# Attention values on quarters of the array, with the keys in block order 3, 2, 0, 1

## The chip, the cores and the metric

The kernel runs on one core of a Trainium2 chip. A core has TensorE (matrix products into PSUM), VectorE, ScalarE and POOL (GpSimd) for the elementwise work, and SyncE (SP), whose queue here issues most DMAs. Each engine takes its instructions in program order. The metric is the device time of one launch in microseconds; the time of a version is the median of several runs. The array of TensorE has 128 rows (contraction) and 128 columns (outputs); an instruction may use all of it, 128 x 64 (a half by columns), or 64 x 64 (a quarter). A float32 product is two matmul instructions.

## The reference

Eight sequences of 256 tokens with 128 features go through a gated cross attention and a gated mixture of experts, both on normalised inputs and added to the input:

```
q = layernorm(x) @ Wq + bq ; k = ctx @ Wk + bk ; v = ctx @ Wv + bv      # 16 heads of 64
scores = q @ k.T / 8 ; masked keys: -1e30 ; keys after the query's position: -1e30
x = x + tanh(g_xattn) * (softmax(scores) @ v @ Wo + bo)
x = x + tanh(g_ffn) * experts(layernorm(x))        # 8 experts 128-512-128, the router's best one
                                                   # does its rows, all others add their constant
```

The context has 1601 keys, but a query at position s sees keys 0 to s only, so the first 256 keys matter. Where every visible key of a query is masked, the softmax is uniform over all 1601 keys. The kernel keeps two extra columns beside the scores for that (`U0`, `U1`, value `NEG_ALL`): their exponentials give the share of the mean value, which `residual` adds.

## The kernel before, in words

**Tiling.** Sequences go in four pairs (`NPAIR`), heads in eight pairs `c` (`NC`). One step `g = 8 * pair + c`, of 32, does two heads of two sequences. All is float32 apart from the bias products, which are bf16. The 256 queries of a sequence are two tiles of 128: tile 0 has blocks 0 and 1 of 64 tokens, tile 1 has blocks 3 and 2, in this order (`load_x`). Keys lie in order 0, 1, 2, 3.

**A step** is software-pipelined over three steps of the loop `for g in range(NG)` (L1254). In iteration `g`:
- `turn(g-2, i)` (L597) transposes the probabilities of head and sequence `i` in three 128 x 128 products and VectorE copies them (L605). Four of them are spread over the step.
- `query(g+1)`, `key(g+1)` (L481, L488): one product of 512 columns each, evicted by ScalarE. `value(g+2)` (L499): the same for the values of four head pairs. These three and others take PSUM banks from the pool `misc` of two.
- `beside_scores` (L1183), after the fourth turn: the product of attention and `wo` of the pair before (`attention_out`, L655), its eviction with the residual (`evict_out`), statistics, transpositions for the next pair, the router.
- `biases(g)` (L516): eight products on quarters of the array put causal and padding biases of query tile 0, and the extra column, into both score banks. `scores(g, b)` (L530) for sequence `b`: eight products on quarters; rows of the array by head `j`, columns by half tile `u`. `tensor_reduce` finds the maximum of tile 0, and two `tensor_tensor_reduce` add the bias to tile 1 and find its maximum (L549, L551).
- `exps(g, 0)` follows scores of sequence 0 at once; `exps(g, 1)` is done in the next iteration, in two parts around the key's eviction (L572). Each exponential instruction is followed by a read of its sum.
- `normalized(g-1, b)` (L583): VectorE's reciprocal and two multiplications on POOL, for both sequences after the third turn.
- `values(g-2)` (L627): the values of both sequences as sixteen instructions of 128 x 64 shape (L616), a head on each half of the array's columns; VectorE adds the bias (L634; ScalarE in the last steps).

Each score bank pair `banks[b]` holds, for each head, columns: an unused one, `U0`, tile 0's scores from `K0` (128), tile 1's from `K1` (256), and `U1`. `U1` and the never visible parts are set once by VectorE's memsets in `plain_constants` (L239 to L242) and stay.

**Order.** All is in an order written out by hand (`tc.manual_schedule()`, L1228). The prologue loads through SP's queue (`load_x`, `load_c`, weights, masks, L124 to L175) and ScalarE's; the sums over the context beyond 256 keys are accumulated by POOL's DMAs (`add_keys`, L154), one after the other in iterations 0 to 6, starting from the load in L164. The epilogue `last_turns` (L1044) ends the last two steps and routes the last pair, beside the planning of the experts' chunks (`plan_full`), and `experts` runs the experts on sorted tokens.

## Time and profile before

| | |
|---|---|
| median of 9 runs | 365.69 us (363.3 to 368.06) |
| the profiled execution | 367.58 us, span 365.9 us |
| TensorE's mean granted clock | 0.985 |
| TensorE busy | 338.3 us |
| VectorE, ScalarE, POOL busy | 248.3, 207.8, 215.8 us |
| span of the loop's steps 0 to 31, first bias product to the last scores | 16.5 to 284 us |
| values (L616, tile o) | 480 instructions, 45.6 us |
| scores (L541) | 1024 instructions, 41.9 us |
| exponentials (L572) | 256, 105.4 us, and as many reads of sums |

How to read it: the page gives the busy time of each engine over the span, and a row of 40 slices with the busy share in tenths. In a timeline a row is start, duration, engine, line, operation, output<-inputs and the number of instructions merged; brackets give the idle time of that engine before it and what ended it. `sc` are the score banks, `o` the values' PSUM tile, `pt` the transposed probabilities, `nmax` the negated maxima, `arena` holds `attT`, the contexts and the weights.

### The profile page before, as it was taken

How to read it: one execution, taken by the hardware profiler on the slowest of the kernel's cores; microseconds unless marked ns; L12 is line 12 of the kernel's file. 1: busy time of each engine (PE TensorE's matmuls, PEld its weight loads, DVE VectorE, ACT ScalarE, POOL GpSimd, SP SyncE). 2: the span in 40 equal slices, each digit the busy share in tenths (PEclk: the TensorE clock that was granted, in tenths of full speed). 3: DMA queues.
4: the chain of work that ended last, by engine and by line, in shares of the span. 5: the costliest groups of instructions: out<-in, count | busy, mean ns of one | idle time of the engine just before them, and what ended most of it. 6: DMA issues, size and time to landing. Idle time of an engine off the chain costs nothing.

```text
span 365.9 us, 9265 instructions
## 1 busy us (share of the span) xinstructions
PE 338.3 (92%) x3244; PEld 238.1 (65%) x3244; DVE 248.3 (68%) x857; ACT 207.8 (57%) x743; POOL 215.8 (59%) x315
## 2 busy tenths in 40 slices
PE   8978799999999999999999999999998698889993
PEld 3434466667667766667766556677577476888893
DVE  3588889785767778887766887756877755724331
ACT  2276587765555757575564875743955414445452
POOL 6065467582365778768764645865848814335654
PEclk9999999999999999999999999999999989989997
DMA  6789666797799994000000000000760039489800
GB/s 182 212 171 205 106 106 102 114 293 229 213 388 383 386 384 175 2 4 1 2 17 0 17 31 1 2 17 2 301 265 17 31 97 322 122 242 364 326 24 15
DMA packets 36472, 53.69 MB, mean 147 GB/s; under 512 B 3946, under 2 KB 22974, under 8 KB 36425
## 3 DMA queue, kind: packets, MB, share of 16 engines
q1 hardware_dynamic: 28280, 44.00, 35.7%
q0 software_dynamic: 7360, 8.73, 12.5%
q8 instruction: 26, 0.43, 0.5%
q10 hardware_dynamic: 784, 0.36, 0.4%
q14 instruction: 22, 0.17, 0.2%
HBM read 27.82 MB, written 25.71 MB: 146 GB/s over the span
## 4 chain that ended last, share of the span: by engine, by line
PE 60%; DVE 16%; DMA 9%; ACT 6%; issue 3%; SPq 2%; POOL 1%; ACTq 0%; POOLq 0%; DVEq 0%
PE pt L603 8%; PE k L491 7%; PE o L616 6%; PE hs L986 6%; PE y L660 6%; DVE sc L551 5%; PE sc L541 5%; PE v L506 5%; PE ys L1002 5%; ACT prob L572 4%; PE q L484 4%; DMA g_sb<-in_g_xattn_dram 2%; DVE nmax L549 2%; DMA arena<-in_ctx_dram 2%; DVE arena L634 2%
## 5 line engine op out<-in xcount | busy, mean ns | idle before, releaser
L572 ACT ACTIVATE prob<-sc,nmax 128x129 f32<-128x129 f32 (+1 forms) x256 | 105.4, 426 | 92.3 <-DVE nmax L551 65.6
L595 POOL TENSOR_TENSOR prob<-prob,rs 128x256 f32<-128x256 f32 (+1 forms) x128 | 104.2, 901 | 58.9 <-DVE rs L586 57.5
L603 PEld LDWEIGHTS pt<-ident,prob 128*128 128x128 f32 x384 | 46.7, 141 | 55.9 <-issue 45.3
L605 DVE COPY probT<-pt 128x384 f32<-128x384 f32 x128 | 67.2, 546 | 11.5 <-PE pt L603 11.1
L603 PE MATMUL pt<-ident,prob 128*128 128x128 f32 x384 | 64.6, 279 | 4.4 <-DVE probT L605 2.9
L551 DVE CUSTOM_DVE_ANT_0 sc<-sc,bias 128x256 f32<-128x256 f32 x128 | 55.3, 432 | 4.5 <-DVE nmax L549 0.2
L572 ACT ACTIVATION_READ_ACCUMULATOR prob<-sc,nmax 128x1 f32 x256 | 53.8, 210 | 0.0
L616 PE MATMUL o<-probT,v 128*64 128x256 f32 x480 | 45.6, 332 | 0.0
L541 PE MATMUL sc<-kT,qT 64*64 64x256 f32 (+3 forms) x1024 | 41.9, 298 | 0.0
L616 PEld LDWEIGHTS o<-probT,v 128*64 128x64 f32 x480 | 29.7, 136 | 16.8 <-issue 7.0
L491 PE MATMUL k<-cT,arena 128*128 128x512 f32 x64 | 35.5, 636 | 4.8 <-DVE arena L634 3.8
L506 PE MATMUL v<-arena,cT 128*128 128x512 f32 x64 | 33.1, 601 | 1.7 <-ACT qT L486 1.6
L484 PE MATMUL q<-xT,arena 128*128 128x512 f32 x64 | 33.1, 598 | 0.1
L541 PEld LDWEIGHTS sc<-kT,qT 64*64 64x64 f32 x1024 | 31.6, 134 | 0.1
L1020 POOL DMA_INDIRECT out_dram<-o,rows x18 | 17.6, 980 | 22.1 <-DVE o L1013 15.9
L549 DVE TENSOR_REDUCE nmax<-sc 128x2 f32<-128x258 f32 x64 | 26.9, 420 | 3.6 <-PE sc L541 3.4
L586 DVE RECIPROCAL rs<-ssum 128x4 f32<-128x4 f32 x64 | 11.1, 173 | 25.1 <-ACT prob L572 22.1
L486 ACT ACTIVATE qT<-q,bqT 128x512 f32<-128x512 f32 x32 | 22.2, 694 | 7.8 <-PE q L484 7.1
L994 ACT ACTIVATE h<-hs,arena 128x128 f32<-128x128 f32 x60 | 17.1, 369 | 14.1 <-issue 7.6
L660 PE MATMUL y<-wo_sb,arena 128*128 128x128 f32 x192 | 23.3, 276 | 0.4 <-DVE zero L370 0.2
L497 ACT ACTIVATE kT<-k,bT 128x512 f32<-128x512 f32 x31 | 21.4, 692 | 2.7 <-PE k L491 2.2
L660 PEld LDWEIGHTS y<-wo_sb,arena 128*128 128x128 f32 x192 | 22.2, 192 | 0.8 <-DVE zero L370 0.8
(242 smaller groups left out, 515.8 us busy)
## 6 DMA issues: line engine op xcount, KB each, us to landing
store<-blank SPq DMA_DIRECT2D x16, 1056.0 KB
arena<-later SPq DMA_DIRECT2D x15, 578.0 KB
rows<-in_ctx_dram POOLq DMA_DIRECT2D x5, 1024.0 KB
later<-ws SPq DMA_DIRECT2D x1, 4624.0 KB
rows<-store SPq DMA_DIRECT2D x23, 132.0 KB
ws<-in_L_ffn_W_dram SPq DMA_DIRECT2D x1, 2048.0 KB
ws<-in_L_ffn_W_dram SPq DMA_DIRECT2D x8, 256.0 KB
rows<-in_ctx_dram SPq DMA_DIRECT2D x1, 1024.0 KB
```

What stands on the lines that cost most here:

```text
L484: nc.tensor.matmul(ps, lhsT=wq_sb[:, c * P : (c + 1) * P], rhs=xT[p], start=True, stop=True)
L491: nc.tensor.matmul(ps, lhsT=wk_sb[:, c * P : (c + 1) * P], rhs=cT[p], start=True, stop=True)
L506: nc.tensor.matmul(ps, lhsT=cT[p][:, t * P : (t + 1) * P], rhs=wv_sb[:, c * P : c * P + 512], start=True, stop=True)
L541: nc.tensor.matmul(s[HB * u : HB * (u + 1), j, at : at + n], lhsT=q[r, lo : lo + HB], rhs=k[r, b * S : b * S + n], start=(t == 1), stop=True,)
L549: nc.vector.tensor_reduce(m[:, 0], s[:, :, U0:K1], AX.X, ALU.max, negate=True)
L551: nc.vector.tensor_tensor_reduce(out=s[:, j, K1:U1], in0=s[:, j, K1:U1], in1=bias[:, 2 * (g // NC) + b], scale=-1.0, scalar=-NEG_ALL, op0= ...
L572: nc.scalar.activation(pr[:, j, lo:hi], s[:, j, lo:hi], AF.Exp, bias=m[:, t, j : j + 1], scale=-1.0 if t else 1.0, accum_out=sm[:, t, j : ...
L595: nc.gpsimd.tensor_tensor(pr[:, :, lo:hi], pr[:, :, lo:hi], r, ALU.mult)
L603: nc.tensor.transpose(ps[:, n * P : (n + 1) * P], pr[:, j, K0 + n * P : K0 + (n + 1) * P], ident)
L605: nc.vector.tensor_copy(pt, ps[:, 0 : 3 * P])
L616: nc.tensor.matmul(o[DK * j : DK * (j + 1), n * P : S], lhsT=v[:, 2 * b + n, cols], rhs=probT[g, 2 * b + j][:, 0:S] if n == 0 else probT[g ...
L660: nc.tensor.matmul(ps[:, i * D : (i + 1) * D], lhsT=attT[p * NC + c][:, t * P : (t + 1) * P], rhs=wo_sb[:, c], start=(c == 0), stop=(c == ...
```

## The change

The keys of a sequence are now stored in block order 3, 2, 0, 1 (contexts and masks are loaded so), which with the query order 0, 1, 3, 2 makes the visible parts contiguous for quarters of the array. `values` splits the contraction as well: rows of the array by the upper or lower 64 keys of a tile (`u`), columns by head. The sums over the two halves of the keys go to two PSUM tiles, `lower` and `upper`, and `joined` puts them together in two steps, one on ScalarE (with the bias, 512 columns) and one on VectorE (an addition of 384 columns, since the upper keys are not seen by query block 0). The values of one sequence are placed ahead of the scores of the first, and those of the other between the scores of both. Iteration 31 keeps the old form for step 29.

`value(g+2)` no longer takes a bank of `misc` but half of the score bank whose exponentials are done. So the constants in these banks do not survive: `biases` writes them anew for each bank, by eight products more in each step (`ends`). Which bank is first alternates (`in_turn`). The maxima are a function of their own; those of the second bank come in the next iteration after the first turn. `beside_scores` becomes `beside_keys` and goes ahead of the third turn; the normalisation of the late bank goes behind the fourth. There are four probability buffers instead of five. `router_places(2)` and the normalisation scales of the attention's output move, and in `last_turns` the maxima and the planning steps.

```diff
--- before.py
+++ after.py
...
+
 HB = P // 2
-BLOCK = ((0, 1), (3, 2))
-
-
-U0, K0, K1, U1, SW = 1, 2, 130, 386, 387
+
+
+U0, K0, U1, K1 = 1, 2, 131, 132
+KE, SW = 130, 388
...
     def load_c(eng, p):
 
-        for b in range(2):
-            eng.dma_start(
-                out=c_sb[p][:, 2 * b : 2 * b + 2], in_=cx[2 * p + b, 0:S, :].rearrange("(t p) d -> p t d", p=P)
-            )
+        load_blocks([eng] * 3, c_sb, cx, p, 1)
+
+    def load_mask(b):
+        for at, lo, n in ((0, P + HB, HB), (HB, P, HB), (P, 0, P)):
+            nc.sync.dma_start(out=mask_sb[:, b, at : at + n], in_=mask[b, lo : lo + n].partition_broadcast(P))
...
-            nc.vector.memset(keys[:, :, U0 : U0 + 1], NEG_ALL)
-
-        for b in range(2):
-            nc.vector.memset(banks[b][:, :, U1 : U1 + 1], -NEG_ALL)
-            nc.vector.memset(banks[b][0:HB, :, K0 + HB : K1], NEG)
-            nc.vector.memset(banks[b][HB:P, :, K1 + 3 * HB : U1], -NEG / 2)
+            nc.vector.memset(keys[:, :, 0 : U0 + 1], NEG_ALL)
+        for lo, hi, v in ((0, HB, NEG), (HB, HB + 2, -NEG_ALL), (HB + 2, 2 * HB + 2, 0.0)):
+            nc.vector.memset(ends[:, lo:hi], v)
 
     def mask_bias(p):
 
         b = slice(2 * p, 2 * p + 2)
...
@@ -496,13 +509,13 @@
         else:
             nc.scalar.activation(kT[g], ps, AF.Identity, bias=bk_c)
 
-    def value(n, engine=nc.scalar):
+    def value(n, engine=nc.scalar, bank=None):
 
         h, t = n // 4, n % 4
         if t == 0:
             vS[h] = p2.tile([P, 4, 512], F32, tag="v", name=f"v_{h}")
         p, c = h // 2, 4 * (h % 2)
-        ps = misc(f"v_{n}")
+        ps = misc(f"v_{n}") if bank is None else bank
         nc.tensor.matmul(
             ps, lhsT=cT[p][:, t * P : (t + 1) * P], rhs=wv_sb[:, c * P : c * P + 512], start=True, stop=True
         )
...
     prob, nmax, ssum, probT = {}, {}, {}, {}
 
-    def biases(g):
-
-        for b in range(2):
-            for u, keys in enumerate(bias0):
-                for j in range(2):
-                    r = slice(HB * j, HB * (j + 1))
+    def in_turn(g):
+
+
+        return (g + 1) % 2, g % 2
+
+    def biases(g, b):
+
+
+        for u, keys in enumerate(bias0):
+            for j in range(2):
+                r = slice(HB * j, HB * (j + 1))
+                n = keys.shape[-1]
+                for at, what, stop in (
+                    (n, ends[r, HB * u : HB * (u + 1) + 2], True),
+                    (0, keys[r, 2 * (g // NC) + b], False),
+                ):
                     nc.tensor.matmul(
-                        banks[b][HB * u : HB * (u + 1), j, 0 : keys.shape[-1]],
+                        banks[b][HB * u : HB * (u + 1), j, at : at + what.shape[-1]],
                         lhsT=ident_bf[r, r],
-                        rhs=keys[r, 2 * (g // NC) + b],
+                        rhs=what,
                         start=True,
-                        stop=False,
+                        stop=stop,
                     )
 
     def scores(g, b):
 
 
-
+        biases(g, b)
         q, k, s = qT[g], kT[g], banks[b]
-        for t, at in enumerate((K0, K1)):
-            for u in range(2):
-                n = HB * (BLOCK[t][u] + 1)
...
+        for t, u, at, lo, n in (
+            (0, 0, K0, P, HB),
+            (0, 1, K0, P, P),
+            (1, 0, K1, 0, S),
+            (1, 1, K1 + HB, HB, S - HB),
+        ):
+            for j in range(2):
...
+
+    def maxima(g, b):
+
+        s = banks[b]
         m = nmax[g, b] = p4.tile([P, 2, 2], F32, tag="nmax", name=f"nmax_{g}_{b}")
-        nc.vector.tensor_reduce(m[:, 0], s[:, :, U0:K1], AX.X, ALU.max, negate=True)
+        nc.vector.tensor_reduce(m[:, 0], s[:, :, U0:KE], AX.X, ALU.max, negate=True)
...
-            prob[g, b] = p5.tile([P, 2, SW], F32, tag="prob", name=f"prob_{g}_{b}")
+            prob[g, b] = p4.tile([P, 2, SW], F32, tag="prob", name=f"prob_{g}_{b}")
...
-    def values(g, o=None):
-        c = g % NC
-        o = misc(f"o_{g}") if o is None else o
-        for b in range(2):
-            values_of(g, b, o[:, b * S : (b + 1) * S])
-        bv_c = bT[:, 2 * NC + c : 2 * NC + c + 1]
-        if g < NG - 4:
-            nc.vector.tensor_scalar(attT[g], o, bv_c, None, ALU.add)
-        else:
-
-            nc.scalar.activation(attT[g], o, AF.Identity, bias=bv_c)
+        att_of(g)
+
+    def values(g, b, lower, upper):
+
+
+
+        v, c = vS[g // 4], g % NC
+        for n, parts in (
+            (1, ((0, 0, S, 0), (1, HB, S, HB))),
+            (0, ((1, P, S, S), (0, P, P + HB, S))),
+        ):
+            for u, lo, hi, at in parts:
+                r = slice(HB * u, HB * (u + 1))
+                for j in range(2):
+                    cols = slice((c % 4) * P + DK * j, (c % 4) * P + DK * (j + 1))
+                    nc.tensor.matmul(
+                        (lower, upper)[u][DK * j : DK * (j + 1), b * S + lo : b * S + hi],
+                        lhsT=v[r, 2 * b + n, cols],
+                        rhs=probT[g, 2 * b + j][r, at : at + hi - lo],
+                        start=(n == 1),
+                        stop=(n == 0),
+                    )
+        for i in (2 * b, 2 * b + 1):
+            probT.pop((g, i))
+
+    def joined(g, lower, upper):
+
+        dst, bv_c = att_of(g), bT[:, 2 * NC + g % NC : 2 * NC + g % NC + 1]
+        nc.scalar.activation(dst, lower, AF.Identity, bias=bv_c)
+        dst, upper = [t.rearrange("p (b s) -> p b s", s=S)[:, :, HB:S] for t in (dst, upper)]
+        nc.vector.tensor_tensor(dst, upper, dst, ALU.add)
...
-        normalized(l, 0)
         turn(g, 0)
+        maxima(l, 1)
         turn(g, 1)
         exps(l, 1)
+        normalized(l, 0)
...
-        plan(9)
+        plan(4)
         turn(l, 0)
         turn(l, 1)
+        plan(5)
...
@@ -1261,21 +1314,26 @@
                     fill(i)
             if p >= 1 and c == 2:
                 residual(p - 1)
+            b0, b1 = in_turn(g)
+            late = b0
+            heads = (2 * b0, 2 * b0 + 1, 2 * b1, 2 * b1 + 1)
             if old is not None:
-                turn(old, 0)
+                turn(old, heads[0])
+            if g > 1:
+                maxima(g - 1, late)
             if new is not None:
                 query(new)
             if g == NC + 1:
                 next(mean)
             if old is not None:
-                turn(old, 1)
+                turn(old, heads[1])
             if g == NG - 1:
 
                 o_old = misc(f"o_{old}")
                 a = Half(0, misc("y_last0")[:, 0:S], banks[0][:, 0, 0:S], banks[1][:, 0])
                 a.out(*range(NC - 4))
             if g > 1:
-                exps(g - 1, 1, 0)
+                exps(g - 1, late, 0)
...
             if g > 1:
-                exps(g - 1, 1, 1)
+                exps(g - 1, late, 1)
             if g == 0:
-                exps(0, 1)
+                exps(0, b1)
+            beside_keys(p, c)
             if old is not None:
-                turn(old, 2)
-            if 1 <= g <= NG:
-                for b in range(2):
-                    normalized(g - 1, b)
+                turn(old, heads[2])
+            if g >= 1:
+                normalized(g - 1, b1)
             if p + 1 < NPAIR and c == 3:
                 ln_scales(f"x{p + 1}")
+            if g + 2 < NG:
+                value(g + 2, bank=banks[b1][:, 0] if g > 0 else None)
+            if g == NC + 1:
+                next(mean)
+            beside_values(p, c)
+            if old is not None:
+                turn(old, heads[3])
+            if g >= 1:
+                normalized(g - 1, late)
+            if p >= 1 and c == (5 if p < NPAIR - 1 else 3):
+                ln_scales(f"y{p - 1}")
...
-            if g + 2 < NG:
-                value(g + 2)
-            if g == NC + 1:
-                next(mean)
-            beside_values(p, c)
-            if old is not None:
...
-            beside_scores(p, c)
...
+            if old is not None and g < NG - 1:
+                lower, upper = misc(f"lower_{old}"), misc(f"upper_{old}")
+                values(old, b0, lower, upper)
             if g > 0:
-                biases(g)
-                scores(g, 0)
-                exps(g, 0)
-                scores(g, 1)
+                scores(g, b0)
+                maxima(g, b0)
+            if g == NG - 1:
+                for b in range(2):
+                    values_of(old, b, o_old[:, b * S : (b + 1) * S])
+                nc.scalar.activation(
+                    attT[old], o_old, AF.Identity, bias=bT[:, 2 * NC + old % NC : 2 * NC + old % NC + 1]
+                )
+            elif old is not None:
+                values(old, b1, lower, upper)
+                joined(old, lower, upper)
+            if g > 0:
+                exps(g, b0)
+                scores(g, b1)
             if g == NC:
                 next(mean)
-            if old is not None:
-                values(old, o_old if g == NG - 1 else None)
             if g == NG - 3:
                 router(2)
+            if g == NG - 2:
+                router_places(2)
             if g == 0:
                 add_keys(g)
```

## The prediction

> **What bounds the kernel now.** I read the page first. TensorE is busy for 92% of the span, no other engine for more than 68%, and the slices put its work at 9 tenths from the seventh slice to the thirtieth, at full clock:
>
> ```profile
> PE 338.3 (92%) x3244; PEld 238.1 (65%) x3244; DVE 248.3 (68%) x857; ACT 207.8 (57%) x743; POOL 215.8 (59%) x315
> ...
> PE   8978799999999999999999999999998698889993
> ```
>
> A busy share does not say that each step is bound by TensorE, so next I took the timeline of TensorE and measured each step from its first bias product (L522) to that of the next step. Steps 2 to 30 are the ones whose values the change touches. Fourteen of them last 8.3 to 12.8 us (step 2 with waits at the start, the others with products beside attention). Fifteen last 6.90 to 7.81 us, 110.98 us together. A long one ends like this:
>
> ```profile
> 174.83 1.02 PE L506 MATMUL v<-arena,cT 128*128 128x512 f32 x2
> 175.69 0.49 PE L603 MATMUL pt<-ident,prob 128*128 128x128 f32 x3
> 176.02 1.95 PE L660 MATMUL y<-wo_sb,arena 128*128 128x128 f32 x16
> 177.81 0.60 PE L455 MATMUL tr_c<-ident,arena 128*128 128x128 f32 x4
> 178.34 0.31 PE L522 MATMUL sc<-bias,ident_bf 64*64 64x66 bf16 x7
> 178.43 0.24 PE L541 MATMUL sc<-kT,qT 64*64 64x64 f32 x1
> ...
> 179.67 1.52 PE L616 MATMUL o<-probT,v 128*64 128x256 f32 x16
> 181.12 0.55 PE L603 MATMUL pt<-ident,prob 128*128 128x128 f32 x3
> ```
>
> The columns are start, duration, instruction. No row has an idle time in brackets: here TensorE's own work is the limit. Biases, scores and values take 2.78 us, 178.34 to 181.12. Then I read all engines over one short step:
>
> ```profile
> 66.04 1.31 PE L541 MATMUL sc<-kT,qT 64*64 64x64 f32 x32
> 66.87 0.43 DVE L549 TENSOR_REDUCE nmax<-sc 128x2 f32<-128x258 f32 x1 [0.19 <-PE sc L541]
> 68.21 0.42 DVE L549 TENSOR_REDUCE nmax<-sc 128x2 f32<-128x258 f32 x1
> 68.47 0.37 ACT L572 ACTIVATE prob<-sc,nmax 128x129 f32<-128x129 f32 x1 [2.02 <-DVE nmax L551]
> 70.18 0.69 ACT L486 ACTIVATE qT<-q,bqT 128x512 f32<-128x512 f32 x1
> 71.50 0.69 ACT L497 ACTIVATE kT<-k,bT 128x512 f32<-128x512 f32 x1
> 72.54 0.47 ACT L572 ACTIVATE prob<-sc,nmax 128x257 f32<-128x257 f32 x1
> 72.91 0.49 PE L522 MATMUL sc<-bias,ident_bf 64*64 64x66 bf16 x8
> 73.18 1.31 PE L541 MATMUL sc<-kT,qT 64*64 64x64 f32 x32
> ```
>
> From scores to scores it is 7.14 us, and a chain fills it: scores and first maxima 2.43 us (66.04 to 68.47), then ScalarE without a gap (four exponentials, q's eviction, two exponentials, k's eviction, two exponentials) to 73.01, and 0.17 us until the biases of the second bank and the scores behind them go. So short steps are bound by this loop, and a shorter product block gives them nothing by itself. Last, the table of waits: k's product waits for VectorE's eviction of the values, 3.8 us, half of it in step 2.
>
> ```profile
> PE k L491 <- DVE arena L634: 3.8, 7, 1.9
> ```
>
> **The change, part by part.** The profiled execution took 367.58 us: 365.9 of span and 1.68 around it. It stands 1.89 above the median of 365.69. The sum is made on 367.58 and moved by 1.89.
>
> *The product block.* Now: 8 biases 0.09 us (178.34 to 178.43), 32 score instructions 1.24 us for 640 columns on each quarter of the array, 16 value instructions 1.45 us for 768 columns on each half. The values become 32 instructions of 640 columns on each quarter, in number and shapes those of the scores. A bank of scores costs 0.62 us by the row, which includes one change of array shape. The starts of single score instructions lie 0.57 apart from bank to bank (178.43, 179.00), so the shape change is about 0.09. Then four such blocks are 4 x 0.57 = 2.28 less 0.04 for the values, which start no bank with 64 columns; the biases double to 16, 0.18 us; filling and leaving the shape costs 0.05 + 0.09, once instead of twice. Sum 2.55, gain 0.23 us. Bounds: with 0.55 for each block 0.27, and with the row's 0.62 and nothing else saved, 2.48 + 0.27, gain 0. I take 0.23, whose row is closest in kind.
>
> *Long steps.* 14 x 0.23 = 3.22 us, plus k's waits in steps 10, 17 and 25 (0.29 each, 0.87): k no longer waits behind both maxima, but for the buffer "upper", freed by the short addition of `joined`. Together -4.09.
>
> *Short steps.* The loop after: the early bank's scores to its maxima and exponentials is again 2.43. ScalarE's new `joined` needs the second batch's values, 1.12 us after the scores, plus some 0.2 to land; with q-like 0.60 it ends at about 1.95, inside the wait for the maxima. VectorE's addition, 384 columns, is estimated at 0.56 from rows of `evict_out` (256 columns 0.425, 128 columns 0.287). VectorE is free at 2.17 (68.21 - 66.04), the addition holds it to 2.67, the turned copy (L605, 0.5) to 3.17, and the late bank's maxima let ScalarE go 1.60 later, at 4.77; it is ready at 4.72. So +0.05, and four more biases per bank ahead of the scores +0.07: 7.14 becomes 7.26. Each short step becomes the greater of 7.26 and its length less 0.23 less its k wait. Over the fifteen that is -1.36 (steps 3, 5, 6, 7, 30 lose 0.11 to 0.36, the others gain 0.13 to 0.34). Ends: floor 7.14 and gain 0.27 give -2.73; floor 7.37 (0.2 us more on VectorE) and gain 0 give +1.0, and the long steps then -4.65 and -0.87.
>
> *`joined` behind a normalisation.* In steps 4, 14, 22 and 28 ScalarE has four L448 instructions (1.65 us) behind v's eviction; they end 1.94 after the scores, joining ends at 2.54, and the exponentials behind it start 0.1 late. q's product, due at 2.27, waits for "lower"; k's and all turns queue behind it on TensorE. 0.15 each, +0.6.
>
> *Hidden.* v's product and eviction in the scores' bank: that bank's exponentials ended at 4.14, the product comes after 4.6; without that cover its wait would be TensorE's, some 0.5 a step. Four probability buffers instead of five: the one reused was turned at the start of the same step. The product with `wo` ahead of v: VectorE's eviction waits for it with nothing ready behind. Normalising one half earlier on POOL: a half takes 1.6 of a step, and turns come a step later. Fewer memsets (0.8 us of VectorE) lie ahead of the first tokens' landing.
>
> *The start.* The contexts' loads go from two DMAs to three per pair (the first pair's on ScalarE's queue, three on SP's), the masks' from two to six, all on SP's.
>
> ```profile
> 9.42 0.33 SPq L132 DMA_DIRECT2D arena<-in_L_xattn_Wv_dram  x1
> 9.79 0.44 SPq L133 DMA_DIRECT2D mask_sb<-in_mask_BxS_bf_dram  x1
> ...
> 13.32 0.47 SPq L164 DMA_DIRECT2D rows<-in_ctx_dram  x1
> ```
>
> On ScalarE's queue one more issue, 0.6, stands before the bias vectors, whose transposition opens TensorE's chain: +0.6 at most if the context lands no earlier. On SP five more issues of 0.4 to 0.6 stand before the context sums' first load (L164), 2.0 to 2.5 us. POOL waits for it, and the normalisations queue behind POOL: those of step 1 start at 32.84 and the first half's turn comes at 36.53, 2.1 us after they end (34.4), so 0 to 0.4 gets through. I take +1.0, between 0 and +3 (the masks' first piece, needed first, is last of three and holds up VectorE).
>
> *The tail.* VectorE takes 4 + 5 planning steps around the last turns instead of nine ahead of them; nine cost TensorE 1.82 us. Against it, the last maxima (1.3) and the first half's reciprocal, behind two copies, move into this stretch: turns up to 2.3 later. Both meet at the same two buffers. I take 0, between -1.8 and +2.3.
>
> Sum: -4.09 - 1.36 + 0.6 + 1.0 + 0 = -3.85: 363.7 on the profiled execution, 361.8 against the median.
>
> **A rule against it.** The row: eight biases start and are through in 0.09 us, 11 ns each, because four quarters work at once. The Trainium skill, "TensorEngine Tiling (Array Packing)", section "Instruction Overhead", counts about 60 cycles for every matmul however few its columns; at the 2.4 GHz that "Trainium Kernel Development and Optimization" gives under "NeuronCore Architecture" an estimate of 25 ns each. By that page sixteen biases alone would take 0.4 us, the block's gain would be 0.01 and the main loop would bring about 1 us instead of 5.45. The trace disagrees for the eight that it shows, so the sum goes by the trace.
>
> **Rivals.**
> - *The loop through ScalarE grows (slower).* ScalarE and VectorE now both handle every step's values, the join is queued ahead of the exponentials, and the addition ahead of the late maxima. For it: the loop has no slack now. Against: the join falls into a 2.02 us wait of ScalarE. It decides from 15F - 110.98 - 4.09 + 1.6 = 0, that is a loop F of 7.57 us, 0.43 over today's. At 7.9 the sum is +5.0: 370.7 against the median.
> - *The block does not shorten (no change).* Two products in a row on one quarter (ends, then keys) may hold up the others. Gain 0 gives -0.75 in the loop, +0.6, +1.0: 366.5.
> - *The start eats it.* At +3 instead of +1: 363.8.
> - *More is gained.* Gain 0.27, floor 7.14, tail -1.8, start 0: -9.2, 356.5.
>
> **How the numbers follow.** The forecast's case, 359 to 364.5, gets 0.42; more gained 0.12; the start 0.12; no shortening 0.12; the loop 0.22. Half of the loop's case lies above 368 and half of the best case below 357.5; leaving out these 0.17 gives the range 357.5 to 368. About 0.5%, 1.8 us, is what a measurement can tell from no change: faster means below 363.9, slower above 367.5. Faster: 0.42 + 0.12 and half of the start's, 0.60; the same: 0.12 and the start's other half, 0.18; slower: the loop's 0.22.
>
> **What would show it.** Values of 64x64 shape, with biases, scores and values in about 2.55 us between turns; long steps 0.2 to 0.5 shorter; short steps at 7.2 to 7.3, with TensorE waiting for exponentials before the biases. The forecast is wrong if short steps pass 7.57, if q waits for "lower" in most steps, or if the first turns of steps 2 and 3 come over 2 us later.

## The result and the profile after

The changed kernel takes 378.88 us (median; 375.79 to 384.65) against 365.27 us: 1.0376 times the time of before, 95% interval 1.0354 to 1.0398. The ratio leaves out runs in a slower state of the chip; 18 runs of the changed kernel remain. The forecast was 361.8, faster. The profiled execution took 376.23 us, with a span of 374.5. It is one of the fastest of the changed kernel, while the profiled execution of before, 367.58, was 2.3 above its median: the two traces show 8.65 us of a difference of 13.6 between the medians.

The page of after, engines, the slices of TensorE and its granted clock, and the costliest part of the chain:

```profile
PE 337.1 (90%) x3964; PEld 242.4 (65%) x3964; DVE 245.8 (66%) x849; ACT 227.1 (61%) x771; POOL 215.7 (58%) x314
...
PE   7868698999999999999999999999998598898993
PEclk9999999998899999999999999999999999989999
...
PE 41%; DVE 17%; ACT 16%; DMA 10%; POOL 7%; issue 6%; SPq 1%; ACTq 1%; POOLq 0%; DVEq 0%
```

TensorE is busy for 1.2 us less than before, so the work did shrink; the span grew by 8.6 us, so waits grew by more. The chain runs over TensorE for 41% of the span, 60% before. The clock row has two slices at 8, from 84 to 103 us, where it had 9.

The answering long step in the timeline of TensorE (start, duration, instruction, in brackets the idle time before it and what ended it):

```profile
179.58 1.02 PE L504 MATMUL k<-cT,arena 128*128 128x512 f32 x2
180.90 2.05 PE L712 MATMUL y<-wo_sb,arena 128*128 128x128 f32 x16 [0.29 <-ACT qT L499]
...
184.41 0.49 PE L633 MATMUL pt<-ident,prob 128*128 128x128 f32 x3
184.83 0.43 PE L674 MATMUL lower<-probT,v 64*64 64x256 f32 x2
...
185.43 0.21 PE L545 MATMUL sc<-ends,ident_bf 64*64 64x66 bf16 x4
185.46 0.24 PE L545 MATMUL sc<-bias,ident_bf 64*64 64x66 bf16 x4
185.49 0.74 PE L567 MATMUL sc<-kT,qT 64*64 64x64 f32 x16
...
187.35 0.55 PE L633 MATMUL pt<-ident,prob 128*128 128x128 f32 x3
```

Two things are to be seen. Biases, scores and values take 184.83 to 187.35, 2.52 us, where they took 2.78. And the product with `wo`, now ahead of v, waits for ScalarE's eviction of q. The table of waits says how often:

```profile
PE pt L633 <- POOL prob L625: 5.5, 6, 2.5
PE y L712 <- ACT qT L499: 2.9, 10, 0.3
...
PE sc L545 <- ACT v L525: 1.2, 1, 1.2
...
PE tr_c L468 <- ACT qT L499: 0.9, 1, 0.9
...
PE lg L747 <- ACT qT L499: 0.6, 2, 0.3
PE n L768 <- ACT qT L499: 0.6, 2, 0.3
```

The second, fourth, fifth and sixth are the same wait for q's eviction and sum to 5.0 us; before none of these products waited for it. Of the first, the waits for POOL's normalisations, 3.1 us fall into the turns of the last step and 1.6 into step 5; before it was 1.5 us, all in the last step.

To find where the time went I took the starts of q's product in both traces, step by step: here, and in the experiments, a step lasts from one q to the next (the prediction counts from first bias product to first bias product). "Before, again" is the kernel before in a second profile (the fifth experiment), with a faster start.

| stretch, us | before | before, again | after |
|---|---|---|---|
| to q of step 6 | 54.55 | 52.47 | 58.73 |
| steps 6 to 8 | 21.71 | 21.70 | 21.37 |
| steps 9 to 11 | 28.52 | 28.51 | 31.50 |
| steps 12 to 30 | 166.92 | 166.59 | 168.11 |
| from q of step 31 to the end | 94.18 | 93.21 | 94.82 |

The start loses 4.2 to 6.3 us, steps 9 to 11 three, and steps 12 to 30, where the block's gain in eleven long steps alone should have brought 2.5 (11 x 0.23), lose 1.2 to 1.5. The three stretches of the loop agree within 0.4 us in both profiles of before, so the experiments are read by them.

### The profile page after: what moved, and what is told of

It is laid out like the page before. It is cut to its first block, busy times and chain, and to the rows that moved or that the text cites. A ratio compares the mean times of both kernels' runs of the same rounds, so it can differ in the third digit from the quotient of the medians.

```text
span 374.5 us, 10703 instructions
## 1 busy us (share of the span) xinstructions
PE 337.1 (90%) x3964; PEld 242.4 (65%) x3964; DVE 245.8 (66%) x849; ACT 227.1 (61%) x771; POOL 215.7 (58%) x314
## 4 chain that ended last, share of the span: by engine, by line
PE 41%; DVE 17%; ACT 16%; DMA 10%; POOL 7%; issue 6%; SPq 1%; ACTq 1%; POOLq 0%; DVEq 0%
ACT prob L602 12%; PE y L712 6%; PE hs L1038 5%; DVE sc L581 5%; POOL prob L625 5%; PE pt L633 5%; PE ys L1054 4%; DMA rows<-in_ctx_dram 4%; PE sc L519 4%; PE sc L567 3%; ACT qT L499 3%; DVE nmax L579 3%; PE lower L674 2%; DVE probT L635 2%; DMA arena<-in_ctx_dram 2%
## 5 line engine op out<-in xcount | busy, mean ns | idle before, releaser
L635 DVE COPY probT<-pt 128x384 f32<-128x384 f32 x128 | 69.5, 549 | 10.4 <-PE pt L633 9.8
L567 PE MATMUL sc<-kT,qT 64*64 64x64 f32 (+3 forms) x1024 | 49.8, 300 | 0.0
L674 PE MATMUL lower<-probT,v 64*64 64x256 f32 x464 | 44.6, 304 | 0.0
L687 ACT ACTIVATE arena<-lower,bT 128x512 f32<-128x512 f32 x29 | 20.0, 689 | 39.1 <-PE lower L674 39.0
L674 PE MATMUL upper<-probT,v 64*64 64x192 f32 x464 | 42.6, 302 | 0.5 <-DVE zero L383 0.5
L674 PEld LDWEIGHTS lower<-probT,v 64*64 64x64 f32 x464 | 32.7, 132 | 6.1 <-issue 2.5
L674 PEld LDWEIGHTS upper<-probT,v 64*64 64x64 f32 x464 | 31.2, 132 | 4.4 <-DVE zero L383 1.4
L519 PE MATMUL sc<-arena,cT 128*128 128x512 f32 x58 | 30.6, 610 | 0.8 <-ACT prob L602 0.8
L567 PEld LDWEIGHTS sc<-kT,qT 64*64 64x64 f32 x1024 | 29.4, 134 | 0.0
L525 ACT ACTIVATE v<-sc 128x512 f32<-128x512 f32 x29 | 17.7, 609 | 17.1 <-PE sc L519 17.1
```

What stands on the lines that cost most here:

```text
L519: nc.tensor.matmul(ps, lhsT=cT[p][:, t * P : (t + 1) * P], rhs=wv_sb[:, c * P : c * P + 512], start=True, stop=True)
L567: nc.tensor.matmul(s[HB * u : HB * (u + 1), j, at : at + n], lhsT=q[r, ql : ql + HB], rhs=k[r, b * S + lo : b * S + lo + n], start=(t == 1 ...
L635: nc.vector.tensor_copy(pt, ps[:, 0 : 3 * P])
L674: nc.tensor.matmul((lower, upper)[u][DK * j : DK * (j + 1), b * S + lo : b * S + hi], lhsT=v[r, 2 * b + n, cols], rhs=probT[g, 2 * b + j][ ...
```

## The experiments

Each result is a ratio to the kernel before, run beside it on the same chip, with its 95% interval in brackets.

**The theory at first.** (a) Five more transfers on SP's queue delay the start; (b) the products with `wo`, moved ahead of v, wait for a PSUM bank; against it (c) that quarters with their join cost time in themselves.

**The loads alone, on the kernel before.** Contexts in three transfers a pair, masks in six in all, in the old layout.

```diff
-        for b in range(2):
-            eng.dma_start(
-                out=c_sb[p][:, 2 * b : 2 * b + 2], in_=cx[2 * p + b, 0:S, :].rearrange("(t p) d -> p t d", p=P)
-            )
+        for at, t, lo in ((slice(0, P), 0, 0), (slice(0, HB), 1, P), (slice(HB, P), 1, P + HB)):
+            eng.dma_start(
+                out=c_sb[p][at, t::2],
+                in_=cx[2 * p : 2 * p + 2, lo : lo + at.stop - at.start].rearrange("b q d -> q b d"),
+            )
...
+    def load_mask(b):
+        for lo, n in ((0, HB), (HB, HB), (P, P)):
+            nc.sync.dma_start(out=mask_sb[:, b, lo : lo + n], in_=mask[b, lo : lo + n].partition_broadcast(P))
```

> The kernel before with the contexts loaded in three pieces instead of two per pair and the masks in six instead of two, in the old layout: only the number of DMA issues of the change. If the later loads are what makes the changed kernel's start slower (its q product of step 6 comes 4.2 us later than before's), this takes 3 to 4.5 us more than before, with the context sums' first load issued about 4 us later. If that delay comes from the new order of work, 0 to 1 us.

Measured: 1.0229 times before (1.0176 to 1.0283), 8.2 us; more than either theory said. q of step 6 starts at 59.18, 4.6 to 6.7 us later than in the two profiles of before, and from there to step 31 every step is as long as before. So the loads alone cost more than half of what the change does, and the start explains 4.6 to 6.7 of the 8.2. It explains nearly all against the profile of a later kernel that was as fast as the one before (1.0002, the mean value's order changed) and whose experts' stage is as long as here: there q of step 6 starts at 52.43, and 6.8 of the 7.0 us between the two spans lie ahead of it. How the start becomes late is to be seen on SP's queue and in POOL's accumulating transfers, of after:

```profile
7.69 1.94 SPq L115 DMA_DIRECT2D mask_sb<-in_mask_BxS_bf_dram  x3
9.68 0.47 SPq L138 DMA_DIRECT2D arena<-in_L_xattn_Wv_dram  x1
10.19 2.54 SPq L115 DMA_DIRECT2D mask_sb<-in_mask_BxS_bf_dram  x3
12.77 3.33 SPq L101 DMA_DIRECT2D x<-in_x_dram  x3
16.14 1.90 SPq L101 DMA_DIRECT2D arena<-in_ctx_dram  x3
18.08 0.60 SPq L170 DMA_DIRECT2D rows<-in_ctx_dram  x1
...
24.29 1.86 POOL L162 DMA_DIRECT2D rows<-in_ctx_dram  x1 [14.06 <-DMA rows<-in_ctx_dram]
35.13 1.59 POOL L162 DMA_DIRECT2D rows<-in_ctx_dram  x1 [5.31 <-DMA rows<-in_ctx_dram]
```

A mask's piece costs 0.65 to 0.85 us to issue, not the 0.44 of the whole before, and even the three transfers of x behind them took 3.33 us instead of 1.85. The first load of the context's sums is issued at 18.08 instead of 13.32; of these 4.8 us the second mask's pieces add 2.1, x's transfers 1.5, the third piece of the contexts 0.8, and what stands ahead of them 0.4. POOL waits for the load until 24.29 (21.05 before), each further accumulation waits for the one before, about ten us apart, and POOL's normalisations are queued in between.

**The products behind the third turn again, alone, on the changed kernel.**

```diff
-            beside_keys(p, c)
             if old is not None:
                 turn(old, heads[2])
+            beside_keys(p, c)
```

> The changed kernel with beside_keys behind the third turn instead of ahead of it. If the products moved ahead wait for q's eviction out of their bank (0.29 us in each of fourteen steps of the changed kernel's profile), that wait goes and it takes 3 to 4 us less than the changed kernel (374.5 to 376). If the wait only shows what the loop through ScalarE needs anyway, 0 to 1 us less.

Measured: 1.0228 (1.0138 to 1.0318), 0.0148 or 5.4 us less than the change: even more than expected. Steps 12 to 30 take 164.20 us instead of 168.11, and the waits of y, logits and places for q's eviction are gone from the table. Nine long steps without other waits (12 to 14, 17, 19, 20, 25, 27, 28) take 82.25 us against 84.36 before (second profile) and 84.83 in the change: 0.23 each less than before. That is the forecast's figure for the product block, but two waits of k for the values' eviction (0.28 each, steps 19 and 27 of before), which the forecast counted apart, are in it; without them 0.17 each is left. New in the table is one wait, which the next experiment but one explains:

```profile
PE upper L674 <- DVE rows L723: 1.8, 1, 1.8
```

**Values on halves, in the places of the quarters, alone.**

```diff
-                lower, upper = misc(f"lower_{old}"), misc(f"upper_{old}")
-                values(old, b0, lower, upper)
+                o = misc(f"o_{old}")
+                values_of(old, b0, o[:, b0 * S : (b0 + 1) * S])
...
-                values(old, b1, lower, upper)
-                joined(old, lower, upper)
+                values_of(old, b1, o[:, b1 * S : (b1 + 1) * S])
+                nc.vector.tensor_scalar(
+                    attT[old], o, bT[:, 2 * NC + old % NC : 2 * NC + old % NC + 1], None, ALU.add
+                )
```

> The changed kernel with the values as sixteen instructions of 128x64 shape again, in the same two places, in one bank evicted by VectorE in one step. The array's shape changes four times a step. If the quarters bring what was reckoned for the product block, this is slower than the changed kernel by 0.3 to 0.5 us in long steps, 6 to 10 us in all (385 to 389). If the quarters themselves or the join cost the time, it is faster than the changed kernel by 3 us or more.

Measured: 1.0329 (1.0248 to 1.0410), in the interval not to be told from the change. In the trace the nine long steps take 86.49 us (84.83 in the change) and eleven short ones 84.47 (82.93), so quarters do shorten the loop; what halves win back elsewhere is unclear here, apart from steps 21 and 22 (20.48 against 21.72). The last experiments ask the same with the rest mended.

**The sums' and gates' loads ahead of the second pair's contexts and wo.**

```diff
+    nc.sync.dma_start(out=ksum, in_=keys_at(SK - TAIL - S))
+    nc.sync.dma_start(out=g_sb[:, 0:1], in_=g_x.partition_broadcast(P))
+    nc.sync.dma_start(out=g_sb[:, 1:2], in_=g_f.partition_broadcast(P))
     load_c(nc.sync, 1)
-    nc.sync.dma_start(out=ksum, in_=keys_at(SK - TAIL - S))
     nc.sync.dma_start(out=wo_sb, in_=wo.rearrange("(c p) d -> p c d", p=P))
-    nc.sync.dma_start(out=g_sb[:, 0:1], in_=g_x.partition_broadcast(P))
-    nc.sync.dma_start(out=g_sb[:, 1:2], in_=g_f.partition_broadcast(P))
```

> The changed kernel with the context sums' first load and the two gates' loads ahead of the second pair's contexts and wo on SP's queue. If POOL's chain of sums, started late, is what delays steps 1 to 5, the sums start 2 to 3 us earlier and the whole takes 2 to 3.5 us less (375.5 to 377). If the start is late for the masks' or the weights' sake, 0 to 1 us less.

Measured: 1.0353 (1.0279 to 1.0427), no difference: a miss. Step 2 is 1.3 us shorter, but other steps of the start take it back (q of step 6 at 59.84). The sums' load was issued 2.0 us earlier (16.13), yet POOL's first accumulation began at 24.13 instead of 24.29: the load did not land sooner. So this order is no cure, and the experiment does not show what an earlier chain of sums would bring; the natural loads below do. The trace shows a chain that the change's own trace had hidden. In time order, the mean value on its way to the residual and VectorE's eviction of y:

```profile
97.48 0.46 SPq L429 DMA_DIRECT2D z_rows<-z  x1
...
101.81 0.35 SPq L430 DMA_DIRECT2D zb<-z_rows  x1
...
106.22 1.19 POOL L697 TENSOR_TENSOR z<-zb,um 128x256 f32<-128x256 f32 x2 [6.17 <-DMA zb<-z_rows]
107.48 1.26 POOL L703 TENSOR_TENSOR x<-x,z 128x512 f32<-128x512 f32 x1
108.78 0.29 DVE L723 TENSOR_TENSOR rows<-y,x 128x128 f32<-128x128 f32 x1 [5.19 <-POOL x L703]
...
109.12 0.38 PE L674 MATMUL upper<-probT,v 64*64 64x192 f32 x2 [2.02 <-DVE rows L723]
```

Before, the same eviction waited 1.99 us for the same sum, but scores and values ran on beside it, since y came later and the values needed one bank, not two. Now y comes earlier, the eviction waits 5.19, and the quarters, whose second bank is y's, wait 2.02 for it. In the change's own profile this wait is missing, since step 10 there was 2.9 us longer for another reason:

```profile
88.00:90.00 2.00, 2.00 (x15) 1.52 (x14) 0.90 (x3) 0.88 (x4) 0.18 (x1) 1.00 0.77 294
90.00:92.00 2.00, 2.00 (x14) 2.00 (x13) 1.14 (x5) 1.38 (x5) 0.00 (x0) 0.62 0.06 17
92.00:94.00 2.00, 2.00 (x8) 1.69 (x9) 0.63 (x2) 0.12 (x2) 0.00 (x0) 0.50 0.95 276
94.00:96.00 2.00, 2.00 (x6) 1.17 (x5) 0.59 (x4) 0.69 (x2) 0.00 (x0) 0.50 0.80 233
96.00:98.00 2.00, 2.00 (x7) 0.49 (x7) 0.59 (x2) 1.34 (x5) 1.27 (x2) 0.67 1.09 310
```

(Stretches of the changed kernel: window, length, busy time and instructions of TensorE, its weight loads, VectorE, ScalarE and POOL, granted clock, DMA share, GB/s.) TensorE works without a pause and its clock is at a half: the products of the mean value with the value weights took 2.90 us instead of 1.85, and k's 1.92 instead of 1.13.

**The kernel before again**, unchanged, for a profile on the chip of the next three.

> The kernel before, unchanged, profiled on the same chip as the three others. If its chain from the first step to the last has the lengths shown before (step 6's q product some 4 us earlier than with the extra loads), the start explains about 4 us of the 8.2 that the extra loads cost; if it is some 8 us shorter in the loop here than in the first profile, the chip explains the rest. I expect a time near 360 to 365 us, and no half clock of TensorE between the 40th and the 280th microsecond.

Measured: 365.14 us. Steps are as long as in the first profile, the start 2.1 us shorter (the table above), the clock full until 291 us. So the start of one kernel differs by 2.1 us between these two profiles.

**The change with natural loads**, the order 3, 2, 0, 1 made on the chip. `swap` is the identity with its halves of columns exchanged.

```diff
-        load_blocks([eng] * 3, c_sb, cx, p, 1)
+        for b in range(2):
+            eng.dma_start(
+                out=c_sb[p][:, 2 * b : 2 * b + 2], in_=cx[2 * p + b, 0:S, :].rearrange("(t p) d -> p t d", p=P)
+            )
...
-        transposed(cT[p], c_sb[p], f"c{p}")
+        ps = misc(f"tr_c{p}")
+        for b in range(2):
+            lo = b * S
+            nc.tensor.matmul(ps[:, lo : lo + P], lhsT=c_sb[p][:, 2 * b + 1], rhs=swap, start=True, stop=True)
+            nc.tensor.transpose(ps[:, lo + P : lo + S], c_sb[p][:, 2 * b], ident)
+        nc.vector.tensor_copy(cT[p], ps)
```

> The changed kernel with contexts and masks loaded as before (two transfers a pair and two in all) and the blocks put in order 3, 2, 0, 1 on the chip: a 128x128 product with a permutation in place of one transposition of each sequence, and five bias operations a pair in place of three. If the transfers on SP's queue cost the changed kernel what they cost the kernel before, the ratio falls from 1.038 by 0.023 to about 1.015, and POOL's first accumulating transfer starts some 3 us earlier. If the changed kernel has its own delay at the start behind which the transfers lie (the rival), it stays above 1.03.

Measured: 1.0208 (1.0160 to 1.0255): 0.0168 or 6.1 us less than the change. q of step 6 starts at 53.88. The sums' load and POOL's first accumulation in this kernel:

```profile
11.05 0.47 SPq L172 DMA_DIRECT2D rows<-in_ctx_dram  x1
...
19.00 1.86 POOL L164 DMA_DIRECT2D rows<-in_ctx_dram  x1 [9.60 <-DMA rows<-in_ctx_dram]
```

The first theory holds in kind: with the transfers gone the start is that of before, and the largest single part of the loss with it. In size it gave 1.015, just below the interval.

**The mean value's three products earlier.**

```diff
+            if g == NC:
+                next(mean)
             if old is not None and g < NG - 1:
                 lower, upper = misc(f"lower_{old}"), misc(f"upper_{old}")
...
                 value(g + 2, bank=banks[b1][:, 0] if g > 0 else None)
-            if g == NC + 1:
-                next(mean)
```

> The changed kernel with the three products of the mean value spread out and earlier: the column sums ahead of step 8's values, the product with the value weights at the end of that iteration, the product with wo behind the next q. Theory: the sums and the product with the weights stand close together, so that TensorE does too little in one stretch and its clock falls to a half for 7 us (3.2 us lost in the profile), and where it does not fall, the eviction of y waits for the mean value (2.0 us in two of the experiments). Then steps 10 and 11 become 3 us shorter: ratio 1.029, clock 1.0 from 90 to 98 us and no wait of the quarters for VectorE's residual eviction in step 11. If the half clock there comes by chance and moves elsewhere, the ratio stays at 1.035 to 1.04.

Measured: 1.0374 (1.0325 to 1.0423): a miss. The wait for the residual is gone, and steps 9 to 11 take 30.96 us instead of 31.50, but the column sums now wait 0.77 for POOL's last sum, and the clock falls to a half all the same (86 to 90 us).

**Natural loads, products behind the third turn and the earlier mean value together**, the three edits above in one kernel.

> The natural loads, the products with wo behind the third turn again, and the earlier mean value together, with the quarters, the join, the block order and the scores' banks as in the changed kernel. If start (8), the wait of these products for q's bank (5) and the mean value (3) are what the change cost, with an overlap of one or two between the last two, it is 13 to 15 us under the changed kernel: ratio 0.995 to 1.003. If quarters and join themselves cost time in the loop (the rival: ScalarE's longer loop), it stays above 1.015.

Measured: 1.0158 (1.0109 to 1.0207). The first theory's range is excluded; the rival's bound of 1.015 lies inside the interval, so the rival is neither shown nor excluded. It is 8.0 us less than the change, where the loads and the products' place alone brought 6.1 and 5.4: these two do not simply add up here. The start is that of before (q of step 6 at 52.75), steps 12 to 30 take 164.72, 1.9 under before; steps 9 to 11 still take 30.81 instead of 28.51, and from q of step 31 to the first product of the experts it is 36.49 instead of 35.26. The first turn of the last step waits there, behind a normalisation that the change had moved back:

```profile
289.59 0.33 PE L645 MATMUL pt<-ident,prob 128*128 128x128 f32 x1 [2.47 <-POOL prob L637]
```

**Another cure for iterations 9 and 10**, on natural loads and products behind the third turn.

```diff
             if new is not None:
                 key(new)
+            if g == NC + 1:
+                next(mean)
...
-            beside_keys(p, c)
+            if g != NC + 2:
+                beside_keys(p, c)
...
+            if g == NC + 2:
+                beside_keys(p, c)
+                o = misc(f"o_{old}")
+                values_of(old, b0, o[:, b0 * S : (b0 + 1) * S])
```

> Natural loads and the products with wo behind the third turn, as in the last experiment, with another cure for the mean value: column sums behind step 8's scores as in the changed kernel, the product with the value weights behind k in place of behind q, and in iteration 10 alone the products with wo behind the fourth turn and the values on halves in one bank, so that no product waits for the residual's eviction there. If the mean value's chain is what still cost 2.3 us in iterations 9 to 11 of the last experiment, steps 9 to 11 together take what they take before (28.5 us, within 0.5) and the ratio goes from 1.016 to 1.010 or less. If the delay is only passed on, steps 9 to 11 stay 1.5 us or more longer than before and the ratio stays at 1.014 to 1.02.

Measured: 1.0057 (1.0013 to 1.0100). The ratio fell as the first theory said and no product waits for the residual's eviction any more, but steps 9 to 11 are still 30.64 us in this profile: two turns in step 11 wait 1.28 and 0.67 for POOL's normalisations, which stand behind the residual's sum in POOL's queue, and the clock is at a half from 106 to 110 us. The time agrees with the theory, the place of the gain does not; the next run's profile has 30.08 there, without these two waits.

**The last normalisation first**, on top of that.

```diff
+        normalized(l, 0)
         turn(g, 0)
         maxima(l, 1)
         turn(g, 1)
         exps(l, 1)
-        normalized(l, 0)
```

> The same, and in the last turns the normalisation of the last step's first half ahead of everything, as in the kernel before. In the last experiment the first turn of the last step waited 2.5 us for POOL there, against 0.8 before. If that order is what the tail costs, the wait falls to about 1 and the time by 1 to 1.7 us: ratio 0.003 to 0.005 below the run beside it. The rival is that the turns then wait for VectorE's planning steps or for the last maxima instead: no difference.

Measured: 1.0016 (0.9968 to 1.0063); the intervals of this and the last overlap, so the gain of 0.004 is not proven. In the trace the turn's wait fell from 2.48 to 0.98 us, and q of step 31 to the first product of the experts is 35.28, as before:

```profile
288.98 0.33 PE L645 MATMUL pt<-ident,prob 128*128 128x128 f32 x1 [0.98 <-DVE nmax L591]
```

**The same with halves in all steps**, by the edit shown for halves above.

> The kernel of the run beside it with the values on halves in one bank and one eviction by VectorE in all steps, in the places of the quarters: what the quarters and the join bring once the start, the products with wo, the mean value and the tail are mended. If the product block's gain of 0.23 us reaches the time in the long steps, this is 2.5 to 4 us slower than the run beside it (ratio 0.007 to 0.011 higher). If ScalarE's and VectorE's part in the join takes the gain back, it is the same or faster.

Measured: 1.0123 (1.0075 to 1.0172), 0.0107 or 3.9 us above the run beside it, with intervals apart: the quarters' gain reaches the time once the rest is mended. The product block of one step, first with quarters, then with halves:

```profile
129.98 0.43 PE L686 MATMUL lower<-probT,v 64*64 64x256 f32 x2
...
132.50 0.55 PE L645 MATMUL pt<-ident,prob 128*128 128x128 f32 x3
```

```profile
128.76 0.87 PE L662 MATMUL o<-probT,v 128*64 128x256 f32 x8
...
131.90 0.55 PE L645 MATMUL pt<-ident,prob 128*128 128x128 f32 x3
```

It is 2.52 us against 3.14. Halves in these places cost more than the 2.78 of before: values and scores alternate and the biases are doubled (which of the two costs it was not separated). So 3.9 us is what quarters are worth in the new order, not against the old one. Against the second measurement of the kernel with quarters, 1.0048 at the end of this section, it is 2.7 us, and there the intervals overlap; in the profiles the steps 6 to 30 differ by 3.3 and 3.4 us. Over steps 12 to 30 quarters in the new order are 2.2 us under before (164.43), and halves 1.1 over it (167.69).

**Is it the order of the thin products that halves the clock?** On the kernel before, the values of step 8 ahead of the column sums, so that sums and product with the value weights stand as close as in the change.

```diff
-            if g == NC:
-                next(mean)
             if old is not None:
                 values(old, o_old if g == NG - 1 else None)
+            if g == NC:
+                next(mean)
```

> The kernel before with one change: step 8's values ahead of the column sums of the mean value, so that only one turn and one q product lie between these sums and the product with the value weights, as in the changed kernel. If this order of thin products (one and eight columns wide) is what brings the half clock there, the profile shows a stretch of half clock between 82 and 95 us, the mean granted clock of the runs falls from 0.992 to about 0.985, and the time rises by 1.5 to 3 us: ratio 1.004 to 1.008. If the half clock follows TensorE's waits instead, which this kernel does not have there, the clock stays at 1.00 and the ratio at 1.000.

Measured: 1.0002 (0.9972 to 1.0032), clock full from 15 to 290 us. This theory of mine fell.

**Is it quarters just ahead of them?** The mended kernel (natural loads, products behind the third turn, mean value spread out, last normalisation first) with halves in iterations 8 to 10 alone; with quarters in iterations 8 and 9 alone and halves elsewhere (the condition reversed); and the mended kernel itself once more beside them.

```diff
+            whole = old is not None and NC <= g <= NC + 2
+            if whole:
+                o = misc(f"o_{old}")
```

> The mended kernel (natural loads, products with wo behind the third turn, mean value spread out, last normalisation first) with the values of iterations 8, 9 and 10 alone on halves, and quarters elsewhere. If quarters followed by the thin products of the mean value make TensorE's clock fall there, the mean granted clock of the runs rises from 0.985 to 0.990 or more, and the time falls by 1 to 2 us against the mended kernel: ratio 0.996 to 0.999. If quarters lower the clock anywhere, the clock stays at 0.985 to 0.987 and the time within 1 us.

> The reverse: the mended kernel with the values on halves in all iterations but 8 and 9, which have quarters. If quarters just ahead of the thin products are what lowers the clock, the mean granted clock of the runs is 0.986 to 0.988, below the 0.993 of all halves, and the profile shows half clock between 82 and 98 us. If it is quarters anywhere, the clock is that of halves, 0.992 to 0.994. The time is that of halves or 1 to 2 us more: ratio 1.010 to 1.015.

> The mended kernel with quarters in all iterations but 10, once more, beside the two others on the same chip: ratio 0.998 to 1.005, mean granted clock 0.985. It is the measure for the two others.

Measured: 1.0133 (1.0089 to 1.0177), 1.0152 (1.0077 to 1.0227) and 1.0048 (1.0017 to 1.0080). The profiles of the first two fit a yes; the stretches around the thin products (columns as above), first with halves at this place, then with quarters there alone:

```profile
86.00:88.00 2.00, 2.00 (x16) 1.62 (x14) 1.41 (x7) 1.57 (x6) 0.00 (x0) 1.00 0.39 116
```

```profile
86.00:88.00 2.00, 2.00 (x6) 1.05 (x5) 1.68 (x7) 1.26 (x5) 0.00 (x0) 0.50 0.14 33
```

Other profiles say no. Halves in all steps of the changed kernel (the third experiment) had a half clock at this place too, from 93 to 100 us; and the mended kernel, with quarters at this place, had it in its first profile (85 to 88 us) and not in its second. The third experiment, then this second profile:

```profile
94.00:96.00 2.00, 2.00 (x5) 0.99 (x5) 1.10 (x4) 0.00 (x0) 0.00 (x0) 0.50 0.96 275
```

```profile
86.00:88.00 2.00, 2.00 (x13) 1.30 (x11) 1.93 (x8) 1.10 (x4) 0.00 (x0) 1.00 0.08 22
```

So quarters ahead of the thin products are neither needed for the half clock nor enough for it. The runs say no as well: with halves at this place the time is 3.1 us longer than that of the mended kernel, not shorter, and the mean granted clock of the runs is 0.987 against 0.989; with quarters at this place alone it is 0.990. What drives the clock stays open, and so does why halves in three iterations cost 3 us in the runs: steps 9 to 11 take 29.14 us in their profile, and 30.08 and 29.08 in the two of the mended kernel. That profiled run, at 367.25 us, is the fastest of its kernel, 3.8 below the median.

No version was faster than the kernel before. The mended one (1.0016 and 1.0048 in two measurements) is level with it or a few tenths of a per cent slower. From q of step 6 to the first product of the experts it takes 251.3 us in both its profiles, against 252.4 and 252.1 before; this gain of about 1 us in the middle of the kernel does not show in the times.

## Why the prediction was wrong

Three terms failed. The place of the product with `wo`, put at nothing, cost 5.0 us of waits, and 5.4 us of time came back when it was undone. The start, +1.0 and at most +3, was 6.1. The short steps, -1.36, were +3.9 in the profiles.

*The product block*: gain 0.23 forecast; 2.78 to 2.52 measured, 0.26. (Its terms add up to 2.56, not 2.55.) The prediction set the rule of the Trainium skill, "TensorEngine Tiling (Array Packing)", section "Instruction Overhead", aside. Added up over all eight biases of a bank the rule does not fit this trace: they and the first score start within 0.06 us (185.43 to 185.49). On a single quarter, which has two of the eight, it does: these two start 0.03 us apart (185.43 and 185.46), near the prediction's estimate of 25 ns.

*Short steps, -1.36*: the loop itself was read rightly; what else waits or stands in the engines' queues was not. Counted as in the prediction, nine of the fifteen came out at 7.07 to 7.53 us, around the forecast floor of 7.26, and in most of them TensorE waits 0.15 for exponentials ahead of the biases. Six took 7.79 to 9.02, and all fifteen 114.9 us instead of 111.0. In step 4 two turns wait 1.6 us for POOL's normalisations (none in the first profile of before, 1.2 in the second); in step 29 a turn waits 0.7 for VectorE's copy; in step 21 a sum of VectorE (L386) stands between the addition of `joined` and the late maxima, and ScalarE waits for these:

```profile
209.36 0.55 DVE L689 TENSOR_TENSOR arena<-upper,arena 128x384 f32<-128x384 f32 x1
209.83 0.59 DVE L386 TENSOR_REDUCE total<-zero 128x32 f32<-128x256 f32 x1
...
212.36 0.37 ACT L602 ACTIVATE prob<-sc,nmax 128x129 f32<-128x129 f32 x1 [0.46 <-DVE nmax L581]
```

Of the 3.9 us, 1.8 lie in steps 29 and 30, and as much comes back behind them: from the first bias product of step 31 to the end it is 82.2 us, before 84.1. The mean of the fifteen, 7.66 us, is past the 7.57 of the rival "the loop grows", so this rival came true in part, by waits and queued work in some steps and not by a longer loop in all. (By the prediction's own rule its step lengths give -1.24, not -1.36.)

*Long steps, -4.09*: the step that failed first. They took 3.8 us more than before, 2.9 of it in the one step that holds the half clock. "The product with `wo` ahead of v: VectorE's eviction waits for it with nothing ready behind" looked at who waits for the product and not at what the product waits for. v had left the pool `misc`, so the next taker of q's bank was no longer v, which stood behind k and a turn (1.3 us from k's start to v's), but this product, directly behind k. It waits 0.29 for q's eviction in most long steps, and other products that now follow k wait up to 0.86, 5.0 us in all, more than the block's gain. With the products moved back, nine long steps gain 0.17 each beside k's waits, somewhat less than the 0.23 forecast.

*"Hidden" once more*: v's product in the scores' bank was to be covered since the exponentials had ended. In step 2 v's own eviction was late and the biases behind it waited 1.2 us. And the same early product made VectorE's eviction wait for the residual's sum of pair 0 (5.2 us in the experiment that shows it, 2.0 before), with the quarters' second bank behind it: 2.0, a wait that was not in the sum.

*The start, +1.0 between 0 and +3*: the mechanism was right, the size was not. Five issues of 0.4 to 0.6 were counted, 2.0 to 2.5 us; the sums' load came 4.8 later, since each piece, and x's transfers behind them, took longer to issue than in the trace of before. The second error was to let only 0.4 through: POOL waits for the chain of accumulations at four places in the first steps (14.1, 5.3, 5.3 and 3.0 us idle), not in step 1 alone. Natural loads bring 6.1 us, and the same loads cost the kernel before 8.2; the upper bound of 3 was far too low, and with it the rival "the start eats it".

*Joining behind a normalisation, +0.6*: not seen. In none of the four steps named does q wait for "lower". Two other products wait 0.2 each for its eviction in the last steps, and k waits 1.8 for the addition in step 4 of the table, as long as it waited there before for the values' eviction (1.9). *The tail, 0*: +0.64 from q of step 31 to the end in the profiles, within its bounds, of which 0.1 lies ahead of the experts; the first turn's wait of 2.5, 0.8 before, was the one foreseen.

*Not in the forecast at all*: the clock. The changed kernel's runs have a mean granted clock of 0.976, those of before 0.992 to 0.995 on the chips of the experiments. The missing share of the clock times the length of the run is 9.2 us in the mean, against 1.8 to 2.8 before; and among the 18 runs in the ratio the time goes up by 0.6 us with each us of it (correlation 0.76). By that, an estimate of some 4 of the 13.6 us goes along with the clock, though whether the clock is cause or effect of the waits is not shown. The single changes moved it too (0.980 with the products moved back, 0.984 with natural loads), so a part of what they brought may be the clock's. In the profile the half clock in step 10 covers 3.4 us of lost TensorE time; for the other runs no trace says where it falls.

Together: 6.1 us for the loads and 5.4 for the products' place, each undone alone, would be 11.5 of the 13.6 us. Undone in one kernel they brought 8.0 with the earlier mean value and 11.6 with the other cure for it, so the split is not exact. The rest, and the gain that the forecast had counted on top of it, lies in the short steps, steps 9 to 11, the tail and the clock, which the mended kernels bring back only together and with overlapping intervals.

## What to carry to other kernels

When a product leaves a shared pool of PSUM banks, list anew who takes each bank and what it then waits for: the next taker inherits the wait that the one that left had covered. A new layout of inputs is paid for in transfers on a queue whose issue times are not constants, and a chain of dependent transfers behind it hands the delay on at each link; making the layout on the chip cost two products a pair in place of two transpositions, two more mask operations a pair, and no time that shows. A piece of work that is moved earlier must be followed to its last operand: here the eviction of y, through POOL and two transfers.

## What was not expected of the hardware

- TensorE's granted clock falls to a half for 6.8 us in the profile of after, and for 3.4 or 6.8 at this place in those of other kernels, while its row shows it busy without a pause (2.00 of 2.00 us in the stretches shown). The Trainium skill, "TensorE: Matmul & The Clock Gate", section "HAM oscillation — how this bites in real kernels", gives as a rule to leave no idle gap of more than about 3.4 us; no such gap stands ahead of this fall (the longest in the 20 us before it is 0.23 us), so here the rule does not cover what the trace shows.
- The experts' stage at the end, whose instructions are the same in all these kernels, varied more than the quarters are worth: in its first layer, the first group of products on the weights in `ws` and the last group of all start 32.1 us apart in one profile and 40.5 in another. First the kernel before with the mean value's order changed, then the mended kernel, whose rows show waits of up to 2 us:

```profile
316.32 1.16 PE L986 MATMUL hs<-xsT,ws 128*128 128x128 f32 x8 [0.38 <-DVE xsT L979]
...
348.40 1.06 PE L986 MATMUL hs<-xsT,arena 128*128 128x128 f32 x8
```

```profile
319.84 1.16 PE L1050 MATMUL hs<-xsT,ws 128*128 128x128 f32 x8 [0.59 <-DVE xsT L1043]
...
357.24 1.35 PE L1050 MATMUL hs<-xsT,arena 128*128 128x128 f32 x8 [1.96 <-DVE xsT L1043]
360.31 1.61 PE L1050 MATMUL hs<-xsT,arena 128*128 128x128 f32 x8
```

  The kernel before, run beside the experiments, goes along with it: 359.6 and 359.8 us beside those whose profiles show 32.1 us for this stretch, 364.7 to 367.1 beside the others (36.4 to 40.5). So ratios to the runs beside them are compared here, not times; but the stretch also differs between kernels run side by side (36.6, 40.5 and 38.8 for the three on one chip), which no experiment explains.
